# A graph-attention layer: attention scores laid with edges along the free dimension, turned by a matrix product quad by quad, and small transfers issued one at a time

## The chip, the cores and the metric

The kernel runs on one NeuronCore of a Trainium2 chip. The time is device microseconds of one execution; it is the median of several runs. The core has a matrix engine (TensorE, PE in the profile), a vector engine (VectorE, DVE), a scalar engine (ScalarE, ACT), a general engine (GpSimd, POOL) and a sync engine (SyncE, SP) that here only issues DMA transfers. All DMA engines of the core are shared by the queues of SP, ACT and POOL. The profile lists the clock that was granted to TensorE as a share of full speed.

## The reference

One layer of graph attention over 12,500 nodes (128 features each) and 200,000 edges, sorted by their target node, with 64 features per edge and four heads of 32:

```python
h = relu(layernorm(x))
hn = (h @ W_node.T).reshape(N, 4, 32)
e  = (edge_attr @ W_edge.T).reshape(E, 4, 32)
att = sum(concat([hn[src], hn[tgt], e], -1) * a, -1)      # [E, 4]
att = where(att > 0, att, 0.2 * att)
m = maximum(segment_max(att, tgt), 0)                     # per node and head
ex = exp(att - m[tgt])
denom = segment_sum(ex, tgt) + (E - deg) * exp(-m)
h_prime = segment_sum((ex / denom[tgt])[:, :, None] * hn[src], tgt)
return x + h_prime.reshape(N, 128)
```

The attention score of an edge is a sum of three terms, each a dot product with a part of `a`: one that depends on the source node, one on the target node and one on the edge's features. So the kernel never forms `e` or the concatenation: it multiplies `a` into the weights once, and adds three scores per edge and head.

## The kernel before

**Tiles.** The edges are cut into 392 *groups* of 512 slots: 511 edges, and a slot 0 that carries the running sum of a node which began in the group before. A slot's place is (column j of 4, partition p of 128). Four groups are a *quad* (98 quads). Between two and four quads are a *super*, over which one softmax runs (two supers of 2 quads, twenty of 4, two of 3, four of 2).

**The head (up to about 120 us).** The nodes' features are normalised, and a product with `wcat` writes a row per node of 137 numbers to `table` in DRAM: 4 x 33 numbers of the projected node, a count, and four source scores (columns 133 to 136, `R_SRC`). Beside it `side` holds the four target scores of a node, each in three bf16 pieces (12 numbers). At the same time GpSimd already gathers rows of raw `x` for the edges of the first four and a half quads (it needs no table for that); these rows are normalised and projected on the chip (`raw_statistics`, `raw_scaled` with L229 on ScalarE, `converted`, `late`, `normed`).

**The gathers.** For each quad GpSimd issues 16 indirect DMAs (`gather`, L141), each of 128 rows by source node, into a ring of eight quads, `ga_all`. Quad q uses slot q % 8, so a gather of quad q + 8 waits until the sums of quad q have read the slot.

**Logits of a group (`logits`).** VectorE builds a one-hot matrix `at` of the target nodes (L537, 80 x 512, bf16): a row for each of the 80 nodes of the group's window, a column for each slot. PE multiplies each 128 columns of it, as weights, with the target scores `pw` of the window (L543, 12 moving columns), and then the edge features `ea` of two columns of slots, as weights, with `wblk` (L546, 8 moving columns, f32), into the tile `lg`, which has edges on partitions: [128, group, j, piece, head]. `lg` has one buffer.

**Sources (`add_sources`).** Once the four groups of a quad are done, `flush` adds the pieces (VectorE, L558) and the gathered source scores (VectorE, L560, which waits for the quad's gathers) into `U`, which holds a super's scores, edges on partitions.

**Softmax of a super (`softmax`).** Four PE transposes (L593) turn `U` into `t_ps`: rows are heads x groups of the super, and the 512 slots lie along the free dimension. ScalarE makes 0.2 x the score (L595); VectorE takes the greater of the two, and finds each node's maximum by segmented scans along the slots (L602, L629, L631); ScalarE takes the exponential, and PE turns the result back (L647).

**Sums of a quad (`sums`).** VectorE multiplies the gathered rows with the weights (`weigh`, L740) and builds a one-hot `hot` of the target nodes (L753). PE sums with three products per group (L758); the fourth (L689) waits for the carry from the group before, which VectorE (L684) and ScalarE (L688) put into slot 0. ScalarE copies the result to `pt` (L690). `divide` (L770 to L784) divides by the denominators and adds `xw`, the window's rows of x; a transfer writes 80 rows of the output (L787). Windows of neighbouring groups overlap, so each of these stores waits until the one before has landed.

**What sets the order.** The order on each engine is written out by hand: under `manual_schedule`, generators are run in turns by `together()`, one step of each at a time. Beside the sums of one quad run the logits of a quad of the next super, and beside them the steps of a softmax. SP's queue is in program order as well: `ea` and `db` (L302 and L304, a quad's edge features, and its targets broadcast to 80 partitions), `pw` (L499) and `xw` (L506), four in a row for a quad, and the stores, four in a row. Their addresses depend on the data: SP loads registers from `base_row` and `base_side` (`windows`, L486) ahead of them.

Of the kernel before, what the change touches and what calls it, by code (L numbers as in the profile page):

```python
# [15 lines left out]
P = 128  # L16
# [10 lines left out]
J = 4  # L27
# [21 lines left out]
def kernel(  # L49
# [39 lines left out]
    assert NT * P == NP >= N + WIN and x.shape[1] == D == P  # L89
# [67 lines left out]
    with tc.manual_schedule():  # L157
# [141 lines left out]
        def fetch_edges(q):  # L299
            g0, m = quads[q]  # L300
            ea = EA[q] = load.tile([P, QG, 2, P], F32, name="ea")
            nc.sync.dma_start(ea[:, :m], edge_t[:, g0:g0 + m])  # L302
            db = DB[q] = load.tile([SPAN, QG, GE], I32, name="db", bufs=2)
            nc.sync.dma_start(db[:, :m, :], dst.rearrange("(g e) -> g e", e=GE)[g0:g0 + m]  # L304
                              .unsqueeze(0).to_broadcast([SPAN, m, GE]))

        with tc.tile_pool(name="node", bufs=2) as node, tc.tile_pool(
# [10 lines left out]
            def indexed():  # L318
                own = index.tile([1, G], F32, name="own")
# [103 lines left out]
            for b, (t0, T) in enumerate(sets):  # L423
                load_nodes(b + 4)
                if b >= len(sets) - 3 and b - len(sets) + 3 < min(2, nq):
                    fetch_edges(b - len(sets) + 3)
# [36 lines left out]
    with tc.tile_pool(name="work", bufs=2) as work, \  # L463
            tc.tile_pool(name="turned", bufs=1) as turned, \
            tc.tile_pool(name="ps", bufs=1, space=bass.MemoryType.PSUM) as ps:
        XW, LG, AT, U, DR = {}, {}, {}, {}, {}
# [26 lines left out]

        def fetch_windows(q):
            g0, m = quads[q]
            pw = PW[q] = load.tile([SPAN, QG, SIDE], BF16, name="pw")
            at = windows(base_side, 2 * SIDE, g0, m)
            for i in range(m):
                nc.sync.dma_start(as_bytes(pw[:, i, :]), rows_at(side, at[i], 2 * SIDE))  # L499

        def fetch_inputs(q):
            g0, m = quads[q]
            xw = XW[q] = work.tile([SPAN, QG, D], F32, name="xw", bufs=3)
            at = windows(base_row, 4 * D, g0, m)
            for i in range(m):
                nc.sync.dma_start(as_bytes(xw[:, i, :]), rows_at(x, at[i], 4 * D))  # L506

        def fetch(q):
            if q not in EA:
                fetch_edges(q)  # L510
# [11 lines left out]
        def open_logits(q):  # L522
# [5 lines left out]
            LG[q] = ps.tile([P, QG, J, PIECES, H], F32, name="lg")  # L528

        def logits(q, i):  # L530
# [5 lines left out]
            sw = PW[q][:, i, :]  # L536
# [4 lines left out]
            for w in range(2):  # L541
                for j in (2 * w, 2 * w + 1):
                    nc.tensor.matmul(lg[:, i, j].rearrange("p k h -> p (k h)"),  # L543
                                     at[:, i, j * P:(j + 1) * P], sw,
                                     start=i + j == 0, stop=False, skip_group_check=True)
                nc.tensor.matmul(lg[:, i, 2 * w:2 * w + 2, 0, :], ea[:, i, w, :], wblk,  # L546
                                 start=False, stop=True, skip_group_check=True)

        def add_sources(q):
# [8 lines left out]
            nc.vector.tensor_reduce(st[:, :m], LG[q][:, :m].rearrange("p g j k h -> p g j h k"),  # L558
                                    AX.X, OP.add)
            nc.vector.tensor_tensor(u, st[:, :m], GA[q][:, :m, :, R_SRC:R_SRC + H], op=OP.add)  # L560
# [10 lines left out]
        def run_on(n):  # L571

            unread = ps.tile([P, QG, J, PIECES, H], F32, name="lg")
            unread = unread.rearrange("p i j k h -> p (i j k h)")[:, 0:P]
            for _ in range(n):
                nc.tensor.matmul(unread, ident, ones, start=True, stop=True)

        def softmax(s):
# [12 lines left out]
            t_ps = ps.tile([SBG * H, GE], F32, name="t_ps")  # L591
            for j in range(J):
                nc.tensor.transpose(t_ps[:R, j * P:(j + 1) * P], u[:, j, :R], ident)  # L593
# [126 lines left out]
        def sums(q):  # L720
# [25 lines left out]
            for i in range(m):  # L746
# [100 lines left out]
        with tc.manual_schedule():  # L847
            for q in range(min(2, nq)):
                fetch(q)
            on_vector = nc.vector.tensor_copy  # L850
# [55 lines left out]
def tile_any_order(ctx, tc, x, src, dst, edge_t, table, side, wblk, ident, part, out, by_tile, E):  # L906
# [29 lines left out]
    pairs = edge_t.rearrange("k g w p -> k (g w) p")  # L936
    src_c = src.rearrange("(c p o) -> c p o", p=P, o=1)
    dst_c = dst.rearrange("(c p o) -> c p o", p=P, o=1)
    with tc.For_i(0, EP // (2 * P), 1) as pair:
        eT = pool.tile([P, 1, P], F32, name="any_eT")  # L940
        nc.sync.dma_start(eT, pairs[:, bass.ds(pair, 1), :])
        lg = psum.tile([P, 2, H], F32, name="any_lg")
        nc.tensor.matmul(lg, eT[:, 0, :], wblk, start=True, stop=True)
        for c in range(2):
            si = pool.tile([P, 1], I32, name="any_si")
            di = pool.tile([P, 1], I32, name="any_di")
            nc.sync.dma_start(si, src_c[bass.ds(pair * 2 + c, 1)].rearrange("c p o -> (c p) o"))
            nc.sync.dma_start(di, dst_c[bass.ds(pair * 2 + c, 1)].rearrange("c p o -> (c p) o"))
# [84 lines left out]
def laid_out(x, src, dst, edge, w_node, w_edge, a):  # L1033
# [22 lines left out]
    et = grouped(edge, 0).reshape(G, 2, 2, P, edge.shape[1]).transpose(2, 4, 0, 1, 3)  # L1056
    et = et.reshape(P, G, 2, P)
# [39 lines left out]
```

## Time and profile before

| what | value |
|---|---|
| median of three runs | 2016.95 us (2013.33 to 2021.75) |
| profiled execution | 2015.89 us, span 2014.1 us |
| mean granted TensorE clock | 0.542 |
| PE, busy | 1366.5 us (68%), 7317 matmuls |
| VectorE, busy | 1343.4 us (67%) |
| POOL, busy | 1506.5 us (75%) |
| ScalarE, busy | 405.6 us (20%) |
| DMA | 279.51 MB, mean 139 GB/s |

The profile is of one execution. An engine's busy time is the sum of its instructions' times; matmuls overlap, since they are pipelined. "Idle before" of a group of instructions is the time for which its engine did nothing ahead of them, and the releaser is what ended it: another engine's instruction, a transfer, or "issue", which means that nothing in the profile was waited for. A line such as L141 is a line of the kernel's source. The slices cut the span into 40 equal parts of about 50 us; each digit is a share in tenths, 9 for 90% or more. An f32 product is recorded as two passes (784 products of L546 are 1568 matmuls).

### The profile page before, as it was taken

The numbers are of one execution on the slowest core, as the hardware profiler recorded it, in microseconds if no ns is written. First come the engines' busy times: TensorE is split into PE (matmuls) and PEld (weight loads), VectorE is DVE, ScalarE is ACT, GpSimd is POOL, SyncE is SP. The second block draws the span as 40 slices with busy tenths as digits, with TensorE's granted clock in tenths as the row PEclk, the third lists the DMA queues.
The fourth block names the chain that finished last, engine by engine and source line by source line (L and its number), as shares of the span: only waits on it lengthen the run. The fifth ranks groups of instructions, "written<-read, shape, count | busy, mean of one in ns | idle before, by whom it ended". The sixth has DMA issues, their size and how long they took to land.

```text
span 2014.1 us, 27314 instructions
## 1 busy us (share of the span) xinstructions
PE 1366.5 (68%) x7317; PEld 1242.7 (62%) x7317; DVE 1343.4 (67%) x3363; ACT 405.6 (20%) x1531; POOL 1506.5 (75%) x1609
## 2 busy tenths in 40 slices
PE   5677888866575766666656666666666575767775
PEld 4566777755565656556656556565566565667664
DVE  7676787766575675766656747656657476768776
ACT  6664111111111111111111111111111111112212
POOL 7777777777777777777777777777777777777774
PEclk9777555555555555555555555555555555555556
DMA  7655676665556565555555555555555555555541
GB/s 251 207 145 117 158 172 149 151 150 145 125 126 149 128 147 142 127 142 134 133 135 132 135 133 134 134 134 133 136 132 134 134 134 134 125 149 127 146 103 31
DMA packets 194093, 279.51 MB, mean 139 GB/s; under 512 B 79849, under 2 KB 143337, under 8 KB 186098
## 3 DMA queue, kind: packets, MB, share of 16 engines
q1 hardware_dynamic: 142128, 165.55, 31.5%
q0 software_dynamic: 50112, 109.61, 24.3%
q10 hardware_dynamic: 1698, 2.58, 0.4%
q8 instruction: 61, 1.00, 0.2%
q14 instruction: 94, 0.77, 0.1%
HBM read 254.25 MB, written 23.30 MB: 138 GB/s over the span
## 4 chain that ended last, share of the span: by engine, by line
DVE 24%; PE 24%; DMA 21%; POOL 9%; issue 9%; SPq 6%; ACT 3%; DVEq 0%; POOLq 0%; ACTq 0%
PE acc L758 12%; DMA out_dram<-res 11%; POOL ga L141 9%; DMA ga<-table,srci 7%; PE lg L546 6%; DVE at L537 5%; DVE res L784 3%; PE acc L689 3%; SPq L499 2%; DVE res L780 2%; DMA xw<-in_x_dram 2%; DVE ga L740 2%; DVE hot L753 2%; DVE ga L684 2%; DVE run L602 2%
## 5 line engine op out<-in xcount | busy, mean ns | idle before, releaser
L141 POOL DMA_INDIRECT ga<-table,srci x1494 | 1419.1, 950 | 455.5 <-issue 382.0
L758 PE MATMUL acc<-ga,hot 128*97 128x137 f32 x2352 | 646.5, 446 | 55.4 <-DVE hot L753 26.7
L758 PEld LDWEIGHTS acc<-ga,hot 128*97 128x97 f32 x2352 | 518.2, 278 | 71.7 <-DVE hot L753 31.6
L543 PEld LDWEIGHTS <-at 80*128 80x128 bf16 x1568 | 212.1, 164 | 515.5 <-DVE at L537 497.5
L543 PE MATMUL lg<-pw,at 80*128 80x12 bf16 x1568 | 169.1, 181 | 441.2 <-DVE at L537 431.4
L546 PE MATMUL lg<-wblk,ea 128*128 128x8 f32 x1568 | 404.4, 355 | 0.0
L546 PEld LDWEIGHTS lg<-wblk,ea 128*128 128x128 f32 x1568 | 376.8, 305 | 0.0
L560 DVE TENSOR_TENSOR U<-st,ga 128x64 f32<-128x64 f32 x98 | 26.5, 270 | 394.1 <-DMA ga<-table,srci 386.8
L537 DVE TENSOR_TENSOR at<-const_ps,db 80x512 bf16<-80x512 f32 x392 | 267.3, 683 | 5.8
L740 DVE TENSOR_TENSOR ga<-ga,ex_ps 128x528 f32<-128x528 f32 x392 | 268.4, 685 | 0.3
L689 PE MATMUL acc<-ga,hot 128*97 128x137 f32 x784 | 257.8, 432 | 3.0 <-ACT ga L688 2.8
L690 ACT COPY pt<-acc 97x137 f32<-97x137 f32 x392 | 107.1, 273 | 723.2 <-PE acc L689 718.1
L689 PEld LDWEIGHTS acc<-ga,hot 128*97 128x97 f32 x784 | 198.8, 283 | 4.8 <-ACT ga L688 4.7
L684 DVE TENSOR_TENSOR ga<-acc,facs 1x132 f32<-1x132 f32 x391 | 115.9, 297 | 126.9 <-ACT pt L690 117.0
L753 DVE TENSOR_TENSOR hot<-const_ps,slot 128x320 f32<-128x320 f32 x384 | 183.5, 478 | 0.0
L688 ACT COPY ga<-acc 1x1 f32<-1x1 f32 x391 | 59.9, 153 | 468.3 <-DVE ga L684 461.1
L141 POOL DMA_INDIRECT ga<-in_x_dram,srci x72 | 69.1, 959 | 23.1 <-issue 16.8
L780 DVE TENSOR_TENSOR res<-pt,const_ps 80x512 f32<-80x512 f32 (+2 forms) x102 | 67.5, 662 | 5.9 <-DMA out_dram<-res 1.6
L784 DVE TENSOR_TENSOR res<-res,xw 80x512 f32<-80x512 f32 (+2 forms) x99 | 67.3, 680 | 6.1 <-DMA xw<-in_x_dram 2.8
L395 PE MATMUL row_ps<-wcat,hT 128*128 128x137 f32 x198 | 37.3, 335 | 21.4 <-DVE tgt L401 10.4
L647 PE MATMUL ex_ps<-ident,ex 64*128 64x64 f32 (+2 forms) x112 | 18.4, 312 | 49.2 <-ACT ex L636 49.2
L558 DVE TENSOR_REDUCE st<-lg 128x64 f32<-128x192 f32 x98 | 35.0, 357 | 23.7 <-PE lg L546 22.7
(138 smaller groups left out, 1025.3 us busy)
## 6 DMA issues: line engine op xcount, KB each, us to landing
db<-in_dst_dram SPq DMA_DIRECT2D x98, 640.0 KB
ea<-in_edge_t_dram SPq DMA_DIRECT2D x98, 512.0 KB
ga<-table,srci POOLq DMA_INDIRECT x1494
xw<-in_x_dram SPq DMA_DIRECT2D x392, 40.0 KB
out_dram<-res SPq DMA_DIRECT2D x392, 40.0 KB
pw<-side SPq DMA_DIRECT2D x392, 1.9 KB
table<-row SPq DMA_DIRECT2D x9, 616.5 KB
xt<-in_x_dram SPq DMA_DIRECT2D x9, 576.0 KB
```

Of the source, the lines that this page charges most:

```text
L141: nc.gpsimd.indirect_dma_start(out=ga[:, i, j, 0:width], out_offset=None, in_=rows, in_offset=bass.IndirectOffsetOnAxis(ap=srci[:, g0 + i, ...
L537: nc.vector.tensor_tensor(at[:, i, :], node_ps[0:SPAN, g0 + i:g0 + i + 1].to_broadcast([SPAN, GE]), db[:, i, :], op=OP.is_equal)
L543: nc.tensor.matmul(lg[:, i, j].rearrange("p k h -> p (k h)"), at[:, i, j * P:(j + 1) * P], sw, start=i + j == 0, stop=False, skip_group_ch ...
L546: nc.tensor.matmul(lg[:, i, 2 * w:2 * w + 2, 0, :], ea[:, i, w, :], wblk, start=False, stop=True, skip_group_check=True)
L684: nc.vector.tensor_tensor(ga[0:1, i, 0, 0:H * HW].rearrange("p (h w) -> p h w", w=HW), before[WIN:WIN + 1, 0:H * HW].rearrange("p (h w) -> ...
L689: nc.tensor.matmul(acc, hot[:, i, 0, :], ga[:, i, 0, :], start=False, stop=True)
L690: nc.scalar.copy(pt[:, i, :], acc)
L740: nc.vector.tensor_tensor(val, val, weight.unsqueeze(3).to_broadcast([P, J, H, HW]), op=OP.mult)
L753: nc.vector.tensor_tensor(hot[:, i, :, 0:SPAN], lane_ps.unsqueeze(1).to_broadcast([P, J, SPAN]), slot[:, g, :].unsqueeze(2).to_broadcast([ ...
L758: nc.tensor.matmul(acc, hot[:, i, j, :], ga[:, i, j, :], start=j == 1, stop=False)
L780: nc.vector.tensor_tensor(res[:, :n, :].rearrange("p g (h d) -> p g h d", d=HD), val[:, :, :, 0:HD], share_ps[0:R, :n, :].unsqueeze(3).to_ ...
L784: add.tensor_tensor(res[:, :n, :], res[:, :n, :], xw, op=OP.add)
```

## The change

There are two parts, and helpers for them.

**Logits.** Edge features now come in another layout: the partitions hold two groups x 64 features, and the 512 slots lie along the free dimension (`ea` is [128, 2, 512] for a quad). `fetch_edges` is cut in two, `fetch_features` and `fetch_targets`. A group's target scores are one bf16 product with `pw` as weights (12 columns used of 32, the rest zero; `pw_all` is a constant tile, cleared once) and `at` as the 512 moving columns, into the rows 32i to 32i + 31 of `lg`, which is now [128, 512]. The edge scores of two groups are one f32 product, with a block matrix `w_edge` as weights and `ea` as the 512 moving columns, into 64 rows.

`add_sources` moves to ScalarE: one copy of the gathered source scores into `U` and one copy of `lg` into `tl`. A PE product with a matrix of zeros and ones, `spread`, adds the pieces and puts the rows of this quad where the super's softmax wants them, in `t_ps`; the quads of a super accumulate there. The four transposes of `U` become four products with the identity that accumulate on top. Nine `spread` matrices, for the place of a quad in a super of two, three or four, are made in the head by a memset and a reduction each on VectorE.

**Transfers.** `pw`, `xw` and the stores are no longer issued four in a row: `fetch_windows`, `fetch_inputs` and `divide` put them on lists (`due`), and `issue` takes one from a list in each step of the logits (`pw`) or of the sums (`xw` and a store). The last three quads issue all that is due at once. `db` of quad q + 2 is issued after the weights at the end of the logits of quad q, where it was issued ahead of them. The rows of a quad's windows are loaded into registers once, for `xw` and the stores both.

The order of GpSimd's gathers is the same, and so are the softmax behind `t_ps`, the sums and the divisions. A fallback for inputs whose groups span more than 80 nodes, which these inputs don't take, is fitted to the new layout.

```diff
+        w_edge = consts.tile([P, 2, P // QG], F32, name="w_edge")
+        SPREADS = {(m, k): consts.tile([P, H, QG * m], F32, name=f"spread{m}{k}")
+                   for m in (2, 3, 4) for k in range(m)}
+        pw_all = consts.tile([SPAN, 3, QG, P // QG], BF16, name="pw")
...
+            nc.vector.memset(w_edge, 0.0)
+            for k in range(2):
+                part_of = slice(half * k, half * (k + 1))
+                nc.vector.tensor_copy(w_edge[part_of, k, 0:H], we_ps[part_of, :])
+            nc.vector.memset(pw_all, 0.0)
...
-        def fetch_edges(q):
+        def fetch_features(q):
             g0, m = quads[q]
-            ea = EA[q] = load.tile([P, QG, 2, P], F32, name="ea")
-            nc.sync.dma_start(ea[:, :m], edge_t[:, g0:g0 + m])
+            pairs = -(-m // 2)
+            ea = EA[q] = load.tile([P, QG // 2, GE], F32, name="ea")
+            nc.sync.dma_start(ea[:, :pairs], edge_t[:, g0 // 2:g0 // 2 + pairs])
+
+        def fetch_targets(q):
+            g0, m = quads[q]
             db = DB[q] = load.tile([SPAN, QG, GE], I32, name="db", bufs=2)
...
             def indexed():
+                for (m, k), spread in SPREADS.items():
+                    nc.vector.memset(spread, 0.0)
+                    nc.vector.tensor_reduce(
+                        spread[:, :, QG * k:QG * (k + 1)],
+                        ident.rearrange("p (i k h) -> p h i k", i=QG, h=H)[:, :, :, 0:PIECES],
+                        AX.X, OP.add)
+                    if k == m - 1:
+                        yield
...
+        due = {"weights": [], "inputs": [], "results": []}
+
+        def issue(*kinds, all_of=False):
+
+            for kind in kinds:
+                for _ in range(len(due[kind]) if all_of else min(1, len(due[kind]))):
+                    nc.sync.dma_start(*due[kind].pop(0))
+
         def fetch_windows(q):
             g0, m = quads[q]
-            pw = PW[q] = load.tile([SPAN, QG, SIDE], BF16, name="pw")
+            pw = PW[q] = pw_all[:, q % 3]
             at = windows(base_side, 2 * SIDE, g0, m)
-            for i in range(m):
-                nc.sync.dma_start(as_bytes(pw[:, i, :]), rows_at(side, at[i], 2 * SIDE))
+            due["weights"] += [(as_bytes(pw[:, i, 0:SIDE]), rows_at(side, at[i], 2 * SIDE))
+                               for i in range(m)]
...
-            at = windows(base_row, 4 * D, g0, m)
-            for i in range(m):
-                nc.sync.dma_start(as_bytes(xw[:, i, :]), rows_at(x, at[i], 4 * D))
+            at = ROWS[q] = windows(base_row, 4 * D, g0, m)
+            due["inputs"] += [(as_bytes(xw[:, i, :]), rows_at(x, at[i], 4 * D)) for i in range(m)]
...
-            LG[q] = ps.tile([P, QG, J, PIECES, H], F32, name="lg")
+            LG[q] = ps.tile([P, GE], F32, name="lg")
...
-            for w in range(2):
-                for j in (2 * w, 2 * w + 1):
-                    nc.tensor.matmul(lg[:, i, j].rearrange("p k h -> p (k h)"),
-                                     at[:, i, j * P:(j + 1) * P], sw,
-                                     start=i + j == 0, stop=False, skip_group_check=True)
-                nc.tensor.matmul(lg[:, i, 2 * w:2 * w + 2, 0, :], ea[:, i, w, :], wblk,
-                                 start=False, stop=True, skip_group_check=True)
+            nc.tensor.matmul(rows_of(lg, i), PW[q][:, i, :], at[:, i, :],
+                             start=True, stop=False, skip_group_check=True)
+            if i % 2:
+                nc.tensor.matmul(rows_of(lg, i - 1, 2), w_edge.rearrange("p k c -> p (k c)"),
+                                 ea[:, i // 2, :], start=False, stop=True, skip_group_check=True)
...
-            st = work.tile([P, QG, J, H], F32, name="st")
-            nc.vector.tensor_reduce(st[:, :m], LG[q][:, :m].rearrange("p g j k h -> p g j h k"),
-                                    AX.X, OP.add)
-            nc.vector.tensor_tensor(u, st[:, :m], GA[q][:, :m, :, R_SRC:R_SRC + H], op=OP.add)
+            nc.scalar.copy(u, GA[q][:, :m, :, R_SRC:R_SRC + H])
+            n = P // QG * m
+            tl = work.tile([P, GE], F32, name="tl")
+            nc.scalar.copy(tl[:n], LG[q][:n])
+            q0, quads_in = supers[s]
+            if q == q0:
+                TL[s] = ps.tile([SBG * H, GE], F32, name="t_ps")
+            spread = SPREADS[quads_in, q - q0].rearrange("p h g -> p (h g)")
+            nc.tensor.matmul(TL[s][:sm * H], spread[:n], tl[:n],
+                             start=q == q0, stop=False, skip_group_check=True)
...
-            t_ps = ps.tile([SBG * H, GE], F32, name="t_ps")
+            t_ps = TL.pop(s)
             for j in range(J):
-                nc.tensor.transpose(t_ps[:R, j * P:(j + 1) * P], u[:, j, :R], ident)
+                nc.tensor.matmul(t_ps[:R, j * P:(j + 1) * P], u[:, j, :R], ident,
+                                 start=False, stop=j == J - 1, skip_group_check=True)
...
                 begun.append((q, i, ga, hot, pt, acc, fc[:, :, g - s0]))
+                issue("inputs", "results")
                 yield
 
         def divide(q, pt, den, lo, hi):
 
+            issue("results", *(["inputs"] if q >= nq - 3 else []), all_of=True)
...
-            at = windows(base_row, 4 * D, quads[q][0] + lo, n)
-            for i in range(n):
-                nc.sync.dma_start(rows_at(out, at[i], 4 * D), as_bytes(res[:, i, :]))
+            due["results"] += [(rows_at(out, ROWS[q][lo + i], 4 * D), as_bytes(res[:, i, :]))
+                               for i in range(n)]
+            if q >= nq - 3:
+                issue("results", all_of=True)
...
             for i in range(QG):
                 logits(q, i)
+                issue("weights")
+                if i == QG - 1 and q + 2 < nq:
+                    issue("weights", all_of=True)
+                    fetch_targets(q + 2)
                 yield
```

In the changed kernel the copy to `U` is L588, the copy of `lg` L591, the product with `spread` L596, the target and edge products L574 and L577, and the four products with the identity L629.

More of the change, by code (lines that the diff above doesn't have):

```diff
@@ L88 @@
     NT = NP // P
-    assert NT * P == NP >= N + WIN and x.shape[1] == D == P
+    assert G % 2 == 0 and NT * P == NP >= N + WIN and x.shape[1] == D == P
     consts = ctx.enter_context(tc.tile_pool(name="consts", bufs=1))
@@ L571, in run_on @@
         def run_on(n):
[L573 to L574 removed]
+            unread = ps.tile([P, GE], F32, name="lg")[:, 0:P]
             for _ in range(n):
@@ L849 @@
                 fetch(q)
+                issue("weights", all_of=True)
             on_vector = nc.vector.tensor_copy
@@ L934, in tile_any_order @@
     nc.vector.tensor_scalar(bound, power, 2.5, None, op0=OP.mult)
[L936 to L944, printed above, removed]
+    src_c = src.rearrange("(g c j p o) -> g c j p o", c=2, j=J, p=P, o=1)
+    dst_c = dst.rearrange("(g c j p o) -> g c j p o", c=2, j=J, p=P, o=1)
+    with tc.For_i(0, EP // (2 * GE), 1) as pair:
+        eT = pool.tile([P, 1, GE], F32, name="any_eT")
+        nc.sync.dma_start(eT, edge_t[:, bass.ds(pair, 1), :])
+        for j, c in [(j, c) for j in range(J) for c in range(2)]:
+            if not c:
+                lg = psum.tile([P, 2, H], F32, name="any_lg")
+                nc.tensor.matmul(lg, eT[:, 0, j * P:(j + 1) * P], wblk, start=True, stop=True)
             si = pool.tile([P, 1], I32, name="any_si")
             di = pool.tile([P, 1], I32, name="any_di")
-            nc.sync.dma_start(si, src_c[bass.ds(pair * 2 + c, 1)].rearrange("c p o -> (c p) o"))
-            nc.sync.dma_start(di, dst_c[bass.ds(pair * 2 + c, 1)].rearrange("c p o -> (c p) o"))
+            for to, of in ((si, src_c), (di, dst_c)):
+                nc.sync.dma_start(to, of[bass.ds(pair, 1), c, j].rearrange("g p o -> (g p) o"))
             dfl = pool.tile([P, 1], F32, name="any_df")
@@ L1054, in laid_out @@
     sources = grouped(src, 0)
-    et = grouped(edge, 0).reshape(G, 2, 2, P, edge.shape[1]).transpose(2, 4, 0, 1, 3)
-    et = et.reshape(P, G, 2, P)
+    et = grouped(edge, 0).reshape(G // 2, 2, GE, edge.shape[1]).transpose(1, 3, 0, 2)
+    et = et.reshape(P, G // 2, GE)
     cols = np.zeros((D, 3, H), a.dtype)
```

11 lines of the change are left out of this document (7 added, 4 removed).

## The prediction

> **What bounds the kernel now.** I read the page first, then the waits, then stretches of the timeline in three places: the steady middle, the start-up and the end. From the page, the slices of POOL and of the clock, and four groups (columns: count, busy us, mean ns of one, idle before and its releaser):
>
> ```profile
> POOL 7777777777777777777777777777777777777774
> PEclk9777555555555555555555555555555555555556
> L141 POOL DMA_INDIRECT ga<-table,srci x1494 | 1419.1, 950 | 455.5 <-issue 382.0
> L543 PE MATMUL lg<-pw,at 80*128 80x12 bf16 x1568 | 169.1, 181 | 441.2 <-DVE at L537 431.4
> L546 PE MATMUL lg<-wblk,ea 128*128 128x8 f32 x1568 | 404.4, 355 | 0.0
> L558 DVE TENSOR_REDUCE st<-lg 128x64 f32<-128x192 f32 x98 | 35.0, 357 | 23.7 <-PE lg L546 22.7
> ```
>
> POOL is "busy" only 75%, but evenly so in every slice but the last: a gather takes 0.94 us and the next starts 0.30 us later, waiting for nothing. 72 + 1494 gathers at 1.255 us are 1965 us of the 2014. The waits say the same from the other side:
>
> ```profile
> POOL ga L141 <- issue: 398.8, 1308, 0.3
> DVE U L560 <- DMA ga<-table,srci: 386.8, 74, 11.8
> ```
>
> VectorE stands 387 us waiting for gathers, in 74 of 98 quads. Sixteen gathers give a quad 20.1 us; PE is busy 13.2 us of that (132.04 us in the 200 us from 900), VectorE 12.7. So only three things move the end: POOL's cadence, a stall of POOL, and what follows the last gather. A stall can come from the ring of 8 quads of gathered rows (slot q%8): the gather of quad q+8 needs the sums of quad q done. In the middle that has 30 to 70 us to spare. At the start it has not:
>
> ```profile
> 119.74 0.27 DVE L560 TENSOR_TENSOR U<-st,ga 128x64 f32<-128x64 f32 x1
> 122.72 3.95 ACT L229 ACTIVATE ga<-ga,shift,rstd 128x128 f32<-128x128 f32 x10
> 130.59 0.59 ACT L595 ACTIVATE low<-t_ps 32x511 f32<-32x511 f32 x1 [1.93 <-PE t_ps L593]
> 241.61 0.66 PE L689 MATMUL acc<-ga,hot 128*97 128x137 f32 x2
> ...
> 244.38 0.94 POOL L141 DMA_INDIRECT ga<-table,srci  x1 [0.30 <-PE acc L758]
> ```
>
> The L689 that ends at 242.3 finishes the first group of quad 4; the gather into its slot (first of quad 12) starts at 244.4: 2.1 us to spare. For quad 1 the four groups have 8.2, 8.4, 9.9 and 6.7 us. So in the first 245 us compute is the critical chain, with POOL just not touched. At the end:
>
> ```profile
> 1967.37 0.94 POOL L141 DMA_INDIRECT ga<-table,srci  x1 [0.30 <-issue]
> 1973.43 0.34 DVE L560 TENSOR_TENSOR U<-st,ga 128x64 f32<-128x64 f32 x1
> 1973.83 1.04 PE L593 MATMUL t_ps<-ident,U 128*32 128x128 f32 x4 [0.43 <-DVE U L560]
> 1974.91 0.59 ACT L595 ACTIVATE low<-t_ps 32x511 f32<-32x511 f32 x1 [1.19 <-PE t_ps L593]
> ```
>
> 46 us follow the last gather: the last softmax, eight groups of sums, and a chain of stores.
>
> **The change, part by part.**
>
> *PE per quad.* A pass of 137 f32 columns starts 0.23 us after the one before (the two of L689 at 1016.94, next matmul at 1017.40, clock 0.5): 1.68 ns a column, so 512 columns are 0.86 us, and an f32 product is two passes (L546: 784 products, 1568 records). Removed: per group four L543 and four L546 passes, 1.00 us (1017.40 to 1018.40). Added per quad: two edge products (L577), 2 x 1.72; one spread product (L596), 1.72; four bf16 products (L574) of one pass. No long bf16 pass is in the trace: its ends are 0.05 us (start to start of the 12-column ones) and 0.86 (an f32 pass); I take 0.43, half the f32 pass for half the bytes. Sum 6.9 us against 4.0: +2.9 us per quad, between 1.4 and 4.6. The Trainium skill (TensorE: Matmul & The Clock Gate, "Back-to-back issue gap") has a pass cost its N moving columns, whatever the rows that come out: that speaks against this change, and would make the bf16 pass 0.427 us, the sum the same; the f32 rows here agree, at two cycles a column and pass.
>
> *The four L593.* They were transposes, one pass each (4 in 1.04 us); they now accumulate, two passes of 128 columns, 8 x 0.215 = 1.7 us: +0.7 per softmax, on its chain.
>
> *VectorE to ScalarE.* VectorE loses L558 and L560 (0.36 + 0.27 us a quad) and the wait for the gather. ScalarE gets the copy to U (nearest row the 128x80 copy L733, 0.33 us) and the copy of lg to SBUF (L268, the same 128x512, 0.58): 0.9 us a quad on an engine that is 20% busy. The wait moves with U: behind it stand the copies L688 and L690 that every group's sums need, and PE's spread product and all its later matmuls. In the middle all of this lies inside 20.1 us: PE 13.2 + 2.9 + 0.2 = 16.3. Cost 0, covered by POOL's cadence; without that cover it would be up to 3 us a quad.
>
> *Start-up.* Here there is no cover. U of quad 0 ran on VectorE at 119.74. On ScalarE it is queued behind the ten L229, which end at 126.67; with the copy of lg, 127.4. PE's spread product and all logits of quad 1 stand behind that (lg is one buffer): 1.7 + 1.7 + 3.5 us, to about 134 where they ended at 125.2. Then hT_e, three L229, the second pair of copies, spread and L593, L595: its end comes at 139.5 to 141.5 instead of 131.2. I take +9. Until the first groups of quad 1 are summed, three quads' edge products add 2 to 4 us, less up to 2 if the clock is higher in the conversion at 160: +12, against 8.2 to spare: POOL first stalls by some 4 us. From 190 to 242 PE was the bound, 2.92 us a group at half clock; there the change is worth between -3.5 (full clock, VectorE's 2.05 us a group then bound) and +4 (half clock, 3.5 a group). At 242: 8.5 to 16 late, less 2.1: a stall of 6.4 to 14 in all. I take 9, as the clock should come up (below). The gathers never make up for it: their cadence is full to the end. The nine memset and reduce pairs before 50 us cost at most 9 x (0.10 + 0.36) = 4.1 us of VectorE, in a stage where ScalarE is 60 to 90% busy; 1 us, inside the 9.
>
> *The end.* U and lg copies (0.9 us, from about 1973.7), spread (0.85 to 1.7) and L593 (0.9 to 1.7) put L595 at 1976.5 to 1978 for 1974.9; one register load less ahead of the last stores gives back 0.5. Between -1 and +6, as the last quads arrive earlier or later; I take +2.5.
>
> *SP.* The same ea, db, pw, xw and out transfers (98, 98, 392, 392, 392), 102 register loads fewer. Stores no longer stand in a row of four, each waiting for the one before (568 us of SP's waits); what was queued behind them comes sooner. xw now comes one per group, the last a group (2.9 us) before L784 needs it, against 0.37 us to issue and 1.5 until such a transfer lands. pw has a quad and more. 0; if xw came late, VectorE would wait inside POOL's cadence. POOL's own order is unchanged.
>
> Sum, on the profiled execution: 2015.9 + 9 + 2.5 = 2027.4. The median of the runs stands 1.1 above that execution: 2028.
>
> **The clock.** In the middle it is granted at 0.50, though PE works without a break for 12 us at a time; from 170 to 180 it was 1.00 at 7.50 us busy of 10, from 190 to 200 0.50 at 8.82. So busy time does not decide. Of a group's 2.92 us only 8 x 0.23 are long streams; L546 streams 8 columns per pass. With 512-column passes it would be some 95%, so I expect a higher clock than 0.542, and PE's surplus largely repaid. The Trainium skill (same page, "What's actually happening") grants the full clock after some 3.4 us of sustained activity; the trace disagrees if activity means busy time.
>
> **Rivals.**
> 1. *Start-up catches up* (not slower). If the clock stands at 1.0 from about 130 on, added passes halve and quads 2 to 7 run at VectorE's pace; stall 0 to 3: 2015 to 2022. For: 1.00 at 170 to 180. Against: PE idles 7 us while ScalarE finishes. It decides where quad 1 is less than 7 us late. By the Trainium skill's rule of the clock (TensorE: Matmul & The Clock Gate, "What's actually happening") it would be this one.
> 2. *PE falls behind at the end.* At half clock the last 13 quads, whose waits for gathers sum to 30.7 us (6.43, 0.53, 3.90, 7.05, 0.87, 3.74, 1.46, 5.81, 0.90 at L560), get 13 x 2.9 + 5 x 0.7 = 41: 10 us late into an end 5 longer, with a stall of 14 or more and a worse lateness from the waits of ScalarE: 2040 to 2055. For: 0.50 all along. Against: the denser streams.
> 3. *Faster.* Only the 46 us at the end can give: at full clock its eight groups save some 4 us, not 10. Under 2007.
>
> **How the numbers follow.** Forecast (stall 4 to 14, end -1 to +6): 2020 to 2037, 0.55; rival 1, 0.23; rival 2, 0.14; faster, 0.04; an unseen queue on SP, 2030 or more, 0.04. 0.5% of 2017 is 10 us, about what a measurement can tell: 2007 to 2027. The forecast lies 0.6 above 2027. Slower 0.33 + 0.14 + 0.04 = 0.51; same 0.22 + 0.23 = 0.45; faster 0.04. From 2015 to 2042 holds the forecast, rival 1 and the edge of rival 2; the likeliest alone is 2020 to 2037.
>
> **What would show it.** POOL's gaps beyond 0.3 us in the stretch from 170 to 260 and none after, some 9 us in all; ScalarE's copy to U waiting for gathers at 74 or more quads, VectorE not at all; PE's clock above 0.542; L595 of the first softmax ending near 140; the last gather near 1977, and 46 to 52 us behind it. It is wrong if POOL has no gap there, if lateness of U behind its gather grows past 5 us in the last quads, or if a gather's 0.94 + 0.30 us changes.

## The result and the profile after

The changed kernel takes 2031.15 us (median of six, 2026.93 to 2032.39), the kernel before 2015.69 us (median of six): a ratio of 1.0074, with a 95% interval from 1.0065 to 1.0084. It is slower by 15 us. In eight of the twelve runs described below the kernel before itself took 2541 to 2561 us, in the other four 2016.55 to 2018.17, and chip 10 was met both ways, so each run is set against the kernel before on the same chip at the same time. The profiled execution took 2029.86 us, with a span of 2027.7 and a mean granted clock of 0.766.

From the page of the changed kernel, the slices of POOL and of the clock, and four groups (columns as before):

```profile
POOL 7776777777777777777777777777777777777773
PEclk8888898677878777777777786777777877877877
L141 POOL DMA_INDIRECT ga<-table,srci x1494 | 1416.8, 948 | 467.4 <-issue 385.9
L596 PE MATMUL t_ps<-tl,spread 128*64 128x512 f32 (+2 forms) x196 | 182.1, 1030 | 477.9 <-ACT tl L591 453.5
L588 ACT COPY U<-ga 128x64 f32<-128x64 f32 x98 | 29.1, 297 | 342.9 <-DMA ga<-table,srci 339.4
L577 PE MATMUL lg<-ea,w_edge 128*64 128x512 f32 x392 | 239.9, 697 | 0.0
L574 PE MATMUL lg<-at,pw 80*32 80x512 bf16 x392 | 180.9, 465 | 3.2 <-DVE at L570 2.9
```

A gather still takes 0.95 us and the next follows 0.30 us later. POOL still sets the pace in every slice but the fourth: there a 7 has become a 6. The clock, 0.5 in most slices before, is now 0.7 to 0.8. The wait for a quad's gathers has moved to ScalarE with U.

The span grew by 13.6 us. Between its gathers POOL stands still 11.9 us longer; the gathers' own durations sum to 2.5 us less (1416.8 + 68.9 for 1419.1 + 69.1); and 50.0 us follow the last gather, for 45.8. The timeline of POOL shows where the 11.9 us are. These are all the gathers with more than 0.45 us ahead of them, but for one at 3 us that both kernels have:

```profile
96.80 0.95 POOL L141 DMA_INDIRECT ga<-table,srci  x1 [3.24 <-DMA table<-row]
190.72 0.94 POOL L141 DMA_INDIRECT ga<-table,srci  x1 [4.14 <-PE acc L726]
196.35 0.94 POOL L141 DMA_INDIRECT ga<-table,srci  x1 [0.95 <-PE acc L726]
208.27 0.94 POOL L141 DMA_INDIRECT ga<-table,srci  x1 [2.24 <-PE acc L726]
214.00 0.94 POOL L141 DMA_INDIRECT ga<-table,srci  x1 [0.87 <-PE acc L726]
256.00 0.94 POOL L141 DMA_INDIRECT ga<-table,srci  x1 [2.37 <-PE acc L726]
```

Less the usual 0.30 each, the first is 2.9 us: it waits for the table's rows. The five others are 9.1 us, and wait for a slot of the ring, that is for the fourth product (L726) of quads 1, 2 and 4. After 256 there is no such gap.

The start-up of the changed kernel on ScalarE, from the timeline:

```profile
124.74 3.95 ACT L238 ACTIVATE ga<-ga,shift,rstd 128x128 f32<-128x128 f32 x10
128.59 0.28 ACT L588 COPY U<-ga 128x64 f32<-128x64 f32 x1
128.74 0.57 ACT L591 COPY tl<-lg 128x512 f32<-128x512 f32 x1
...
136.11 0.58 ACT L277 COPY hT_e<-acc 128x512 f32<-128x512 f32 x1 [6.59 <-PE acc L275]
...
142.21 0.59 ACT L632 ACTIVATE low<-t_ps 32x511 f32<-32x511 f32 x1 [3.73 <-PE t_ps L629]
```

U of quad 0 starts when the ten normalisations (L229 before, L238 here) are done, 8.9 us later than on VectorE before. The first softmax's 0.2 x product ends at 142.8, for 131.2 before. The end, from the timeline, all engines:

```profile
1976.81 0.94 POOL L141 DMA_INDIRECT ga<-table,srci  x1 [0.30 <-issue]
...
1983.24 0.30 DVE L721 TENSOR_TENSOR ga<-acc,facs 1x132 f32<-1x132 f32 x1
1983.57 0.15 ACT L725 COPY ga<-acc 1x1 f32<-1x1 f32 x1 [3.10 <-DVE ga L721]
1984.48 0.27 ACT L727 COPY pt<-acc 97x137 f32<-97x137 f32 x1 [0.76 <-PE acc L726]
1984.78 0.30 ACT L588 COPY U<-ga 128x64 f32<-128x64 f32 x1
1984.94 0.58 ACT L591 COPY tl<-lg 128x512 f32<-128x512 f32 x1
...
1985.57 1.92 PE L596 MATMUL t_ps<-tl,spread 128*32 128x512 f32 x2 [1.12 <-ACT tl L591]
...
1988.82 0.58 ACT L632 ACTIVATE low<-t_ps 32x511 f32<-32x511 f32 x1 [3.31 <-PE t_ps L629]
```

U of the last quad waits on ScalarE behind L725, which waits for VectorE's carry, and behind L727, which waits for PE's product with that carry: 7.0 us after the last gather, for 5.1 before. From U's start to L632's are 4.0 us, for 1.5 to L595 before. Together that is 4.5 us; what follows is the same (38.3 us for 38.6).

### The profile page after: what moved, and what is told of

Its sections match the earlier page's. It is cut to its first block, busy times and chain, and to the rows that moved or that the text cites. A ratio compares the mean times of both kernels' runs of the same rounds, so it can differ in the third digit from the quotient of the medians.

```text
span 2027.7 us, 23725 instructions
## 1 busy us (share of the span) xinstructions
PE 1323.0 (65%) x5273; PEld 737.9 (36%) x5273; DVE 1299.2 (64%) x3189; ACT 476.1 (23%) x1727; POOL 1504.1 (74%) x1609
## 4 chain that ended last, share of the span: by engine, by line
PE 36%; DMA 18%; POOL 17%; issue 12%; DVE 9%; ACT 6%; SPq 0%; ACTq 0%; DVEq 0%; POOLq 0%
POOL ga L141 17%; DMA ga<-table,srci 16%; PE acc L795 12%; PE t_ps L596 8%; PE lg L577 5%; PE lg L574 5%; PE acc L726 3%; PE t_ps L629 2%; ACT tl L591 2%; DVE at L570 1%; DVE ga L777 1%; ACT U L588 1%; ACT ga L238 1%; DVE stats L216 1%; DVE hot L790 1%
## 5 line engine op out<-in xcount | busy, mean ns | idle before, releaser
L141 POOL DMA_INDIRECT ga<-table,srci x1494 | 1416.8, 948 | 467.4 <-issue 385.9
L795 PE MATMUL acc<-ga,hot 128*97 128x137 f32 x2352 | 461.6, 343 | 77.5 <-DVE hot L790 44.4
L596 PE MATMUL t_ps<-tl,spread 128*64 128x512 f32 (+2 forms) x196 | 182.1, 1030 | 477.9 <-ACT tl L591 453.5
L795 PEld LDWEIGHTS acc<-ga,hot 128*97 128x97 f32 x2352 | 357.2, 201 | 270.2 <-ACT ga L770 74.9
L727 ACT COPY pt<-acc 97x137 f32<-97x137 f32 x392 | 107.1, 273 | 681.1 <-PE acc L726 675.5
L577 PE MATMUL lg<-ea,w_edge 128*64 128x512 f32 x392 | 239.9, 697 | 0.0
L596 PEld LDWEIGHTS t_ps<-tl,spread 128*64 128x64 f32 (+2 forms) x196 | 25.6, 188 | 504.9 <-ACT tl L591 504.3
L726 PE MATMUL acc<-ga,hot 128*97 128x137 f32 x784 | 184.5, 322 | 3.3 <-ACT ga L725 3.3
L574 PE MATMUL lg<-at,pw 80*32 80x512 bf16 x392 | 180.9, 465 | 3.2 <-DVE at L570 2.9
L635 DVE TENSOR_TENSOR t_ps<-t_ps,low 64x511 f32<-64x511 f32 (+2 forms) x28 | 19.3, 689 | 213.2 <-ACT low L632 213.1
L726 PEld LDWEIGHTS acc<-ga,hot 128*97 128x97 f32 x784 | 133.8, 197 | 11.2 <-ACT ga L725 9.3
L588 ACT COPY U<-ga 128x64 f32<-128x64 f32 x98 | 29.1, 297 | 342.9 <-DMA ga<-table,srci 339.4
L574 PEld LDWEIGHTS <-pw 80*32 80x32 bf16 x392 | 37.8, 97 | 195.0 <-issue 178.6
L725 ACT COPY ga<-acc 1x1 f32<-1x1 f32 x391 | 59.9, 153 | 187.1 <-DVE ga L721 183.0
L141 POOL DMA_INDIRECT ga<-in_x_dram,srci x72 | 68.9, 956 | 23.2 <-issue 18.0
L577 PEld LDWEIGHTS lg<-ea,w_edge 128*64 128x64 f32 x392 | 42.0, 151 | 59.7 <-issue 59.2
```

The source lines that it names most:

```text
L141: nc.gpsimd.indirect_dma_start(out=ga[:, i, j, 0:width], out_offset=None, in_=rows, in_offset=bass.IndirectOffsetOnAxis(ap=srci[:, g0 + i, ...
L574: nc.tensor.matmul(rows_of(lg, i), PW[q][:, i, :], at[:, i, :], start=True, stop=False, skip_group_check=True)
L577: nc.tensor.matmul(rows_of(lg, i - 1, 2), w_edge.rearrange("p k c -> p (k c)"), ea[:, i // 2, :], start=False, stop=True, skip_group_check ...
L596: nc.tensor.matmul(TL[s][:sm * H], spread[:n], tl[:n], start=q == q0, stop=False, skip_group_check=True)
L726: nc.tensor.matmul(acc, hot[:, i, 0, :], ga[:, i, 0, :], start=False, stop=True)
L727: nc.scalar.copy(pt[:, i, :], acc)
```

## The experiments

### The two copies on VectorE (three runs)

```diff
-            nc.scalar.copy(u, GA[q][:, :m, :, R_SRC:R_SRC + H])
+            nc.vector.tensor_copy(u, GA[q][:, :m, :, R_SRC:R_SRC + H])
...
-            nc.scalar.copy(tl[:n], LG[q][:n])
+            nc.vector.tensor_copy(tl[:n], LG[q][:n])
```

> The changed kernel with its two copies, of the source scores to U and of lg to tl, on VectorE where add_sources was before; all else as changed. In the changed kernel's profile U of quad 0 starts at 128.6 (119.7 before), right behind the ten L238 of ScalarE, POOL then stalls 9.1 us between 190 and 256, and U of the last quad waits on ScalarE until 1984.8 behind L725. Theory A (ScalarE's queue makes the start-up late): U of quad 0 back near 120 to 123, the stalls from 190 to 256 down to 0 to 4 us, U of the last quad 2 to 4 us nearer to its gather; span 2017 to 2023 for 2027.7. Rival B (PE's longer passes make it late): the stalls stay at 7 to 10 us and the span at 2025 to 2029. The stall of 2.9 us at the first gather from the table, at 96.8, stays in both.

> The same kernel as the first experiment (both copies of add_sources on VectorE), on another chip if there is one where the kernel before takes some 2016 us: the first four ran on a chip where it took 2541 us and ScalarE and SP stood still for up to 13 us at a time. Theory A (ScalarE's queue makes the start-up late): U of quad 0 near 120 to 123 for 128.6, POOL's stalls from 190 to 256 down from 9.1 to 0 to 4 us, span 2017 to 2023. Rival B (PE's longer passes): stalls of 7 to 10 us, span 2025 to 2029. The stall of 2.9 us at the first gather from the table stays in both.

> Copies on VectorE, long head as in the change. Where the kernel before takes some 2016 us, between the changed kernel (1.0072) and that with both edits (1.0005): the loss at the first gather from the table stays at 3 to 6 us, the stalls after it are 0 to 2 us, 46 to 48 us follow the last gather, ratio 1.001 to 1.003. If the head's delay is handed on to later stalls, these are 4 us or more and the ratio is 1.004 or more. Where it takes some 2550 us: the first two looks at this kernel gave 0.986 and 1.001; 0.985 to 1.002.

The third run met a chip with 2017.1 us for the kernel before, and gave 1.0013 (1.0004 to 1.0022), 2020.34 us. Its timeline, POOL and VectorE:

```profile
98.33 0.94 POOL L141 DMA_INDIRECT ga<-table,srci  x1 [4.66 <-DMA table<-row]
...
124.04 0.24 DVE L588 COPY U<-ga 128x64 f32<-128x64 f32 x1
124.15 0.68 DVE L591 COPY tl<-lg 128x512 f32<-128x512 f32 x1
```

The loss at the first gather from the table stays (4.4 us). Behind it no gather has more than 0.45 us ahead of it: the 9.1 us of stalls are gone. All of PE's longer passes are still there, so they alone do not make these stalls; the copies' place on ScalarE has to come to them. The 4.4 us were not handed on to later stalls either. Of the end, 49.1 us follow the last gather, more than the 46 to 48 expected; 1.7 of them come after L632 (40.0 for 38.3 us) and are not explained.

In the first two runs the kernel before took 2541 and 2561 us, and the ratios were 0.986 (0.981 to 0.991) and 1.001 (0.998 to 1.003). There POOL has gathers with more than 0.45 us ahead of them in 95 and in all of the 98 quads, so these runs say nothing of the start-up. That one kernel gave two ratios that differ by 1.5% on two such chips was not explained.

### A short head (three runs)

Eight of the nine spread matrices are made by a small copy of the first one's block; five of them beside the logits of quad 1, three much later.

```diff
             def indexed():
-                for (m, k), spread in SPREADS.items():
-                    nc.vector.memset(spread, 0.0)
-                    nc.vector.tensor_reduce(
-                        spread[:, :, QG * k:QG * (k + 1)],
+                block = SPREADS[2, 0]
+                nc.vector.memset(block, 0.0)
+                nc.vector.tensor_reduce(
+                    block[:, :, 0:QG],
...
+        def spreads(*sizes):
+            for (m, k), spread in SPREADS.items():
+                if m in sizes and (m, k) != (2, 0):
+                    nc.vector.memset(spread, 0.0)
+                    nc.vector.tensor_copy(spread[:, :, QG * k:QG * (k + 1)],
+                                          SPREADS[2, 0][:, :, 0:QG])
+                    yield
```

> The changed kernel with one memset and one reduction for the spread matrices in the head, where nine of each were; the other eight are made by a memset and a small copy each, five beside the logits of quad 1 and three much later. Theory A (VectorE's nine pairs delay the table): the first gather from the table starts at 94 to 95 without the extra wait of 2.9 us; and since conversion and logits follow the same head, the later stalls come no larger than 9 us: last gather 2 to 3 us earlier, span 2024 to 2026. Rival B (the later start-up is not delayed by the head, so that the gap at 96.8 only took part of the later stall in advance): the gap goes, the stalls from 190 to 256 grow by up to 2.9 us, and the span stays at 2027 to 2029. Rival C (the table was late for another reason): the gap at the first gather from the table stays.

> The same kernel as the second experiment (one memset and one reduction in the head for nine of each), on another chip if there is one. Theory A: the stall of 2.9 us at the first gather from the table goes, the later ones stay at 9 us or less, span 2024 to 2026. Rival B: the stall goes and the later ones grow by as much; span 2027 to 2029. Rival C: the stall stays.

> The shorter head alone (copies of add_sources on ScalarE as in the change), where the kernel before takes some 2016 us. On the chip of the last two runs the changed kernel lost 5.6 us at the first gather from the table and 10.8 us between 149 and 260, and 50.0 us followed the last gather; with both edits it lost 0.5 us, none, and 46.9 us. If the two causes are apart: the loss at the first gather from the table is 0 to 1 us, that from 149 to 260 stays at 8 to 11 us, 49 to 51 us follow the last gather, and the ratio is 1.004 to 1.006. If the head's delay was handed on to the later stalls: they fall to 4 to 7 us and the ratio to 1.003 or less.

In all three the kernel before took 2541 to 2561 us, and the ratios were 1.0166 (1.0139 to 1.0193), 1.0149 (1.0116 to 1.0182) and 1.0147 (1.0115 to 1.0178). What they were made for, the start-up at POOL's own pace, they can't show: in the first of them POOL lost 22.5 us at the first gather from the table. So the shorter head alone was not measured where the kernel before takes some 2016 us. They are of use below, as the partner of the next kernel. What the engines do in such a run, from the timeline of the first of them (its lines are one less from `indexed` on):

```profile
1008.95 0.70 SPq L549 DMA_DIRECT2D dr<-in_dst_rows_dram  x1
...
1011.05 0.70 SPq L312 DMA_DIRECT2D ea<-in_edge_t_dram  x1
...
1013.27 0.59 ACT L631 ACTIVATE low<-t_ps 64x511 f32<-64x511 f32 x1 [13.42 <-remote]
...
1015.14 0.95 POOL L141 DMA_INDIRECT ga<-table,srci  x1 [5.04 <-PE acc L725]
```

ScalarE does nothing for 13.4 us, though PE's products that it needs were done at 1002.3. In the same stretch, from 1001 to 1013.2, SP takes 0.70 us for nine of its thirteen instructions, a move of a register too: 302 moves, loads and waits of SP took 0.64 to 0.76 us in this trace, none in that of the changed kernel. VectorE and PE wait for ScalarE, and POOL for a slot. So in this stretch POOL does not set the pace. These traces hold a quarter of the semaphore events (13,855 for 53,921), so their releasers are not to be relied on. What freezes the engines was not found.

### Both edits (two runs)

> Both edits: copies on VectorE, and one memset and reduction in the head. If the two causes add up as in theory A of each: no stall at the first gather from the table, 0 to 4 us from 190 to 256, and an end 0 to 3 us longer than that of the kernel before: span 2014 to 2020, the time within 0.3% of before. If PE's longer passes are a cause of their own, 2022 or more remains.

> Copies on VectorE and the shorter head. Where the kernel before takes some 2016 us: theory A, no stall at the first gather from the table, 0 to 4 us of stalls from 190 to 256, ratio 0.999 to 1.003; rival B (PE's passes), stalls of 7 us or more there and a ratio of 1.004 or more. Where it takes some 2550 us: 0.995 to 1.002, as on the chip before.

In the second run, where the kernel before took 2016.55 us: 2017.45 us, a ratio of 1.0005 (0.9995 to 1.0014). Its timeline, POOL, VectorE, PE and ScalarE (lines one less from `indexed` on):

```profile
94.42 0.94 POOL L141 DMA_INDIRECT ga<-table,srci  x1 [0.78 <-issue]
...
120.48 0.23 DVE L587 COPY U<-ga 128x64 f32<-128x64 f32 x1
...
1969.51 0.21 DVE L587 COPY U<-ga 128x64 f32<-128x64 f32 x1
...
1970.61 1.92 PE L595 MATMUL t_ps<-tl,spread 128*32 128x512 f32 x2
...
1974.27 0.59 ACT L631 ACTIVATE low<-t_ps 32x511 f32<-32x511 f32 x1 [3.28 <-PE t_ps L628]
```

The gap of 0.78 is the only one over 0.45 us, but for the one at 3 us. U of quad 0 is back at 120.5. So the two edits give back all that the change cost, within the measurement, though its products, its layout, its accumulation and its way of issuing transfers are all still there. The end is still 1.2 us longer in this trace (47.0 for 45.8); the gathers' own durations, 1485.3 us for 1488.2, make up for it.

In the first run the kernel before took 2561.09 us: 0.9998 (0.9974 to 1.0021), 2558.76 us, on the same chip as the second run of the short head alone, 2598.7 us. The two differ only in the engine of the copies: 39.9 us, 0.41 us in each of 98 quads. That is what the place on ScalarE costs on that chip, where POOL's pace does not cover it. It is not one number: on chip 5 the copies on VectorE with the long head took 2512.23 us and the copies on ScalarE with the short head 2584.68, which is 72 us, or 0.74 us a quad, with the head in it as well.

### The changed kernel again

> The changed kernel itself, for comparison on the same chip as the next run. Where the kernel before takes some 2016 us: ratio 1.006 to 1.009 as measured. Where it takes some 2550 us, as on the two chips of the first seven experiments: there compute sets POOL's pace, so both the copies on ScalarE (1.5% between the sixth and the seventh experiment) and the passes count in every quad: ratio 1.013 to 1.022, at or a little above the 1.015 and 1.017 of the kernel with the shorter head.

On the same chip as the second run of both edits: 2031.44 us, 1.0072 (1.0056 to 1.0089). The loss at the first gather from the table was 5.6 us there, that from 149 to 260 10.8 (9.6 of it from 193 on, behind L726), and 50.0 us followed the last gather.

### One pass for the spread product

```diff
-        SPREADS = {(m, k): consts.tile([P, H, QG * m], F32, name=f"spread{m}{k}")
+        SPREADS = {(m, k): consts.tile([P, H, QG * m], BF16, name=f"spread{m}{k}")
...
-            tl = work.tile([P, GE], F32, name="tl")
+            tl = work.tile([P, GE], BF16, name="tl")
```

> The changed kernel with tl and the spread matrices in bf16, so that the spread product is one pass and the scores lose bits (a measurement of time: the precision of the target and edge scores is left out). Theory A (ScalarE's queue): only the pass goes, 0.43 to 0.86 us a quad on PE: U of quad 0 stays at 128 to 129, the stalls from 190 to 256 fall by 1 to 3 of 9.1 us, the tail by 0.5 to 1; span 2024 to 2027. Rival B (PE's passes are the cause): each of the eight quads that stand between the start and the stall at 256 saves 0.43 to 0.86, so the stalls fall by 4 us or more and the span to 2022 or less.

The kernel before took 2541.22 us there: 1.0040 (1.0015 to 1.0065), 2550.22 us. The kernel with the short head took 2584.68 on that chip. PE is busy with the spread product for 53.5 us, for 170.7 in that kernel, and the copy to `tl` takes 0.58 us in both. So the one pass less, with its operands in bf16, is worth some 34 us, 0.35 us a quad, and more if the long head costs something there. PE's passes do count once the cover is gone. The spans that were expected don't apply, and whether one pass less would shrink the stalls of the start-up was not measured.

### The transfers alone, on the kernel before

The lists `due`, the later `db` and the registers loaded once, as in the diff of the change, put into the kernel before.

> The kernel before with only the second part of the change: pw, xw and stores from lists, one per step, db behind the weights, registers loaded once. Forecast: no stall of POOL beyond 0.3 us, last gather within 1 us of 1968.3, tail within 1 us of 45.8, ratio to before between 0.999 and 1.001. Rival: db or xw come late at the start-up or at the end; then VectorE waits for them and the time goes up by 2 us or more.

The kernel before took 2541.22 us there, and the ratio is 0.9992 (0.9973 to 1.0011): no difference that can be told. The interval is nearly twice as wide as the forecast's range, and the last-gather figures can't be compared.

### A version meant to beat both

The end of 46 us is the one stretch that POOL doesn't bound, so a shorter last super was tried, on the kernel before.

```diff
-    ends = [2, 2], [3, 3, 2, 2, 2, 2]
+    ends = [2, 2], [3, 3, 2, 2, 2, 1, 1]
...
-        FREE = 2
+        FREE = 1
```

> The kernel before (without the change), with its last super of two quads cut into two of one quad, and the one-hot matrices of only the last quad, for the last two before, left to GpSimd. Only what follows the last gather should change: four groups of sums stand behind the last softmax where eight did. In the kernel before, the last eight groups took from 1986.6 to about 2003, so four save at most some 8 us. Theory: the tail of 45.8 us falls to 37 to 42, and the time by 4 to 9 us (ratio 0.9955 to 0.998). Rival: the sums of the last but one quad now stand beside the last softmax on VectorE, and push it back by what they save: ratio 0.999 to 1.001. POOL's gathers stay without stalls in both. Where the kernel before takes some 2550 us, the same saving of 4 to 9 us is within what 5 rounds can tell, ratio 0.996 to 0.999.

2026.87 us, for 2018.17 on the same chip: 1.0042 (1.0028 to 1.0055), slower. VectorE's timeline (the U is that of the last quad):

```profile
1994.25 0.27 DVE L560 TENSOR_TENSOR U<-st,ga 128x64 f32<-128x64 f32 x1
...
1997.62 1.21 DVE L602 TENSOR_TENSOR_SCAN run<-kp,t_ps 16x511 f32<-16x511 f32 x1
```

The rival was right, and worse than it said. What follows L595 fell from 38.6 to 28.6 us, as hoped. But U of the last quad came 21.9 us after the last gather (at 1972.4) for 5.1. A scan over 16 rows takes 1.21 us, as one over 32 did: this step of a softmax of half the rows costs VectorE as much as that of a whole one. So there was one more softmax to fit into the last quads, with four one-hot matrices of 0.48 us that VectorE now builds where GpSimd did, and the sums of the quads before stand ahead of the last. Which of the two parts of the edit costs how much was not measured apart. The chip was another than that of the profile before.

## Why the prediction was right, by its steps

**The bound** held: POOL's 0.95 + 0.30 us, with nothing lost after 256 us. Only the start-up and the end moved the time, as the three things named said.

**Start-up.** The copy to U was to be queued behind the ten L229, which it was (128.59, right behind L238). L595 was to end at 139.5 to 141.5; it ended at 142.8, of which 2.0 arose ahead of the queue, as the ten L238 were late (124.74 for 122.72). A stall of 6.4 to 14 us, 9 taken, was forecast from 170 to 260 (the sum of the range takes 4 as the least, without a reason); 9.1 were measured, at 190 to 256, and 9.6 in the second trace of the same kernel. The third run on VectorE shows that the copies' place on ScalarE is what makes the stall: the same passes without it, and no stall. The forecast had put part of the 12 us of lateness down to added edge products, and that fits: the first L726 of quad 1 ends at 190.45, for 175.76 (L689) before, 14.7 us late; with the copies on VectorE it ends at 181.84, with both edits at 179.00. So some 8.6 us are the copies' place, some 3 the head, and some 3 what stays of the change, which the 8.2 us to spare cover. The traces are of different chips, so a microsecond either way is not to be read.

**The head** was mis-sized, and put in the wrong place. The nine pairs were costed at 1 us "inside the 9". VectorE is busy with them for 3.1 us, from 35 to 40. POOL loses 2.9, 5.6 and 4.4 us in the three traces with the long head and 0.5 us in the one with the short head, on the same chip as the 5.6: the table's rows land later, and the gather that switches from `x` to `table` waits for them. In the kernel before that gather started without a wait, and how near it was to one was not worked out for the prediction. What the head costs in the end is not settled: with the copies on VectorE the long head has 1.0013 (1.0004 to 1.0022), the short one 1.0005 (0.9995 to 1.0014), on two chips; the difference is some 1.6 us, and the intervals overlap.

**The end** was put at +2.5, from -1 to +6; it is +4.2. The term that was short is the lateness of U: no allowance was made for the copies L725 and L727, with their waits, that stand ahead of it on ScalarE (1.9 us). The chain from U to L632 was put at 1.6 to 3.1 us longer, and is 2.6.

**The sum** came nearer than its terms, and that is luck. Start-up and head cost 12.0 us for the 9 forecast, the end 4.2 for 2.5; but the gathers' own durations are 2.5 us shorter, which nothing had forecast, so that the span grew by 13.6 for 11.5. In all four traces of the changed kernel and its variants where the kernel before takes some 2016 us they sum to 1485.3 to 1485.8 us, for 1488.2 before and 1492.0 in the variant with the shorter last super; why, no run shows. The text also sets its 2028 at 0.6 above 2027, where it is 1; nothing hangs on that.

**The middle** cost nothing, though a sign that the prediction had named as speaking against it came up: in quads 91 to 94 U lies 7.3, 8.8, 5.3 and 7.3 us behind its gather, past 5 us (5.3, 4.6, 2.3 and 3.1 before), and ScalarE waits for gathers in 56 quads and not in 74 or more. The cover was thinner than stated. It still held: from quad 10 on a slot of the ring is free 44 us or more before the gather that takes it (39 to 91 us in the kernel before, where the text has 30 to 70). Without the cover the move to ScalarE costs 0.41 us a quad on one chip and some 0.74 on another, for the 3 us stated as the most for all of it.

**Prices and clock.** A pass of 512 f32 columns was put at 0.86 us; the median from start to start is 0.91 at a clock of 0.5 and 0.48 at 1.0. The bf16 pass, put at 0.43, is 0.54 and 0.32. PE is busy 130.8 us of the 200 from 900, for 132.0: the higher clock repaid the added passes. The rise came with fewer, longer streams at nearly the same busy time, which bears out that recorded busy time alone doesn't decide. The Trainium skill (TensorE: Matmul & The Clock Gate, "What's actually happening") ties the clock to how busy the array has been recently; read as recorded busy time, neither kernel agrees (0.51 at 132.0 us of 200, 0.72 at 130.8), and no run here shows what it counts.

**Rivals.** The start-up did not catch up. The condition for it, a clock of 1.0 from about 130 on, was not met: it was 0.67 to 0.92 in the stretches of 10 us from 130 to 180, and 1.00 only from 180 to 200. PE did not fall behind at the end: after 256 us no gather has more than 0.45 us ahead of it. That rival went by half clock, and the clock from 900 to 1100 was 0.72. SP has no queue that shows: with both edits the kernel has its transfers as changed and no loss.

## What to carry to other kernels

When one engine's cadence covers all, a change is worth what it does in the few stretches without cover: look for the smallest margins of the buffers that this engine waits for, at the start-up above all, and ask what stands ahead of the moved instruction on its new engine just there. An engine that is 20% busy on average can be full for 10 us at the one place that counts. And a one-time set-up is not free because it is short: it delays whatever switches on in the head.

## What the runs showed that had not been expected

Where the kernel before took 2541 us and more, ScalarE stood still for 13.4 us although what it needed was done, and SP took 0.70 us for a move; why is not known. Another part of the change counts there: with the short head and the copies on ScalarE it loses 1.5 to 1.7%, twice what the whole change loses where POOL sets the pace. And a scan over 511 columns takes 1.21 us for 16, 32 and 64 rows alike.
